# Reordering the steps of an attention and deformable-convolution kernel, with eleven gather buffers in place of ten

## The chip, the cores and the metric

The kernel runs on one core of a Trainium2 chip. Time is device microseconds (us) from the start to the end of one execution, lower is better. Five engines matter: TensorE (PE in the profile, its weight loads PEld), VectorE (DVE), ScalarE (ACT), GpSimd (POOL), which here does nothing but issue indirect DMAs, and SyncE (SP), which issues the plain DMAs.[...]

## The reference

`x` has shape (8, 256, 64, 64) in float32. Two layers follow each other, both of the form `x = x + layer(group_norm(x))`, with 32 groups of 8 channels.

```python
# layer 0: local attention, 4 heads, 3x3 neighbourhood
qkv = einsum('oc,bchw->bohw', w_qkv, x); q, k, v = split(qkv, 3)
logits[b,h,kk,l] = sum_d q[b,h,d,l] * patch3x3(k)[b,h,d,kk,l]
attn = softmax(logits, axis=kk)
kernel[b,h,kk,l] = sum_c w_kg[h,kk,c] * qkv[b,h,c,l] + b_kg[h,kk]   # generated weights
out = w_proj @ (alpha * sum_kk kernel * patch(v) + beta * sum_kk attn * patch(v))

# layer 1: modulated deformable 3x3 convolution
om = conv3x3(x, w_off) + b_off              # 18 offsets and 9 masks a pixel
v  = bilinear sample of x at the 9 shifted places (4 corners each), times sigmoid(mask)
out = einsum('bckhw,ock->bohw', v, w)
```

## The kernel before

**Tiles.** An image is worked on in 8 chunks (`NC`) of 8 rows, 512 pixels each (`N`), with 256 channels as two halves of 128 partitions (`NT`). The current image lies in SBUF as `image`; its value after layer 0 is also stored to DRAM as `kept`.

**Layer 0** is the generator `attention(b)` (L550). It computes the group statistics (`Norm` and `ready`), normalises chunk by chunk (`normed`, tile `xn`), and takes seven steps a chunk, each ended by a `yield`. In step 1 `spread_weights` (four matmuls `wk`, each followed by a DVE multiply L483) belongs to the chunk before, called `d`, and `q(0)`, `q(1)` (L276) belong to this one. Step 2 is `k`, step 3 `products` (the DVE multiply `qk` L354) and half of `weighted`, step 4 logits and `generated`, step 5 `v(0)` and `turned` (`gt`, L398), step 6 `v(1)`, the projection's first half and `softmax_3`, step 7 the projection's second half, `second_stats`, `weights` (transposes of the weights, L462) and `keys(0)` (transposes of v, L498). All of them take PSUM tiles from one pool of four, `ps_a`.

**Between the layers** the generator `prepare(b)` (L617) writes the normalised image to a DRAM table (`to_table`, L629 to L638), computes the offsets (`om`, L649), turns them into table indices and corner weights (`positions`, tiles `idx` and `wt`), loads the next image chunk by chunk, and takes its first statistics (`first_stats`, L258).

**Layer 1** is a loop of slots: one slot is one of the 9 kernel taps of one chunk, so 72 slots an image (`SLOTS`) and 576 in all. A slot needs four blocks of 128 pixels. A block is gathered by an indirect DMA of 128 rows of 4 KB (`gather`, L764, POOL), its first corner is scaled on ACT (`scale`, L780), and the other three are added on DVE (`sum_corners`, L788, three instructions a block). Then PE transposes the block (`transposes`, L815), ACT copies it out of PSUM (L818), and PE multiplies it by the tap's weights into `po` (`product`, L832). After the ninth tap, `finished` (L840) adds `po` to the residual `r` on DVE (L843, two instructions) and stores the result. `po` has a single buffer, so the first product of the next chunk has to wait until `finished` has read it.

**The order.** PE, ACT, DVE and POOL run in the order in which the program is written out by hand (`manual_schedule`). The call `ahead(i)` issues the scaling of blocks i+8 and i+9, the sums of blocks i+6 and i+7, and two gathers. Gathers run `LEAD` = 18 blocks ahead, and only 14 ahead in the last image (`LAST_GATHERS`); they land in a pool of 10 buffers. The loop body for slot n is:

```python
transposes(n); ahead(4 * n)
product(n - 1)
# steps of attention / prepare of the next image, 73 over 72 slots
if the product was a chunk's last: finished(...)
ahead(4 * n + 2)
```

All 73 steps of image 0 and six steps of image 1 (`STEPS + STEPS_AHEAD`) run before the loop; the loop then stays six steps ahead of the image.

Of the kernel before, what the change touches and what calls it, by code (L numbers as in the profile page):

```python
# [58 lines left out]
def preact_kernel(ctx: ExitStack, tc: tile.TileContext, a: dict, out: bass.AP):  # L59
# [75 lines left out]
    for t in xn2:  # L135
        nc.gpsimd.memset(t, 0.0)

    kt = const.tile([P, NT, R + 2, WP], F32, tag="k", name="k")
    vt = const.tile([P, NT, TC, KT, KT], F32, tag="v", name="v")


    w_effT = const.tile([P, NT, HEADS, KK], F32, tag="w_effT", name="w_effT")
    nc.vector.tensor_scalar(bkg, bkg, alpha, None, ALU.mult)
    with (
        tc.tile_pool(name="prep", bufs=1) as prep,
        tc.tile_pool(name="prep_ps", bufs=1, space=PSUM) as prep_ps,
    ):
        ps = prep_ps.tile([P, NT, HEADS, KK], F32, tag="eff", name="eff")
        for ct in range(NT):
            for h in range(HEADS):  # L150
                for i in range(2):
                    nc.tensor.matmul(
                        ps[:, ct, h, :],
                        w_qkv[h // 2][:, 2 * (h % 2) + i, ct * P : (ct + 1) * P],
                        w_kgT[:, 2 * h + i, :],
                        start=(i == 0),
                        stop=(i == 1),
                    )
        for ct in range(NT):
            nc.vector.tensor_scalar(  # L160
                w_effT[:, ct], ps[:, ct], alpha, None, ALU.mult
            )
# [29 lines left out]
    class Norm:  # L192


        def __init__(self, stats, name):
            self.name = name
            mv = p1.tile([P, NT, 2], F32, tag="mv", name=f"mv_{name}")
            for ct in range(NT):
                nc.vector.bn_aggr(mv[:, ct, :], stats[:, ct].rearrange("p c s -> p (c s)"))
            ps = psum_a(f"gn_{name}")  # L200
            nc.tensor.matmul(ps[:, 0:NT], gmat, mv[:, :, 0], start=True, stop=True)
# [48 lines left out]
        return t[:, ct, dy : dy + R, dx : dx + W]  # L250

    stats0: dict = {}

    def first_stats(b, c):
        if c == 0:
            stats0[b] = p2.tile([P, NT, NC, 6], F32, tag="stats0", name=f"stats0_{b}")
        for ct in range(NT):
            nc.vector.bn_stats(  # L258
                stats0[b][:, ct, c, :], image[:, ct, c * N : (c + 1) * N]
            )  # L260

    class Attention:

# [34 lines left out]
                    vt[:, :, :, R : R + 2, :].rearrange("p c t y x -> p (c t) (y x)"),  # L298
                )

        def keyed(self, which, i, to):

            for lo, hi in [(0, 2)] * (self.c == 0 and i == 0) + [(2 + 4 * i, 6 + 4 * i)]:
                for m in range(NT):
                    ps = psum_a(f"ps{'qkv'[which]}_{self.u}_{lo}_{m}")
                    o = which * C + m * P
                    for ct in range(NT):
                        nc.tensor.matmul(  # L308
                            ps[:, : (hi - lo) * WP],
                            w_qkvT[:, ct, o : o + P],  # L310
                            self.xn[:, ct, lo:hi, :],
                            start=(ct == 0),
                            stop=(ct == NT - 1),
                        )
                    to(m, lo, hi, ps)

        def k(self, i):
            self.keyed(
                1,
                i,  # L320
                lambda m, lo, hi, ps: nc.scalar.copy(  # L321
                    kt[:, m, lo:hi, :].rearrange("p r w -> p (r w)"), ps[:, : (hi - lo) * WP]
                ),
            )

        def v(self, i):
            self.keyed(
                2,
                i,
                lambda m, lo, hi, ps: nc.scalar.copy(vt[:, m, :, lo:hi, :], tiled(ps, hi - lo)),  # L330
            )

        def products(self):

# [41 lines left out]
        def generated(self):  # L376

            ps = psum_a(f"gen_{self.u}")
            n = HEADS * KK
# [8 lines left out]
            self.gs = gs = p1.tile([P, N], F32, tag="gs", name=f"gs_{self.u}")[:n]  # L388
            nc.scalar.copy(
                gs.rearrange("p (t y x) -> p y t x", y=T, x=T),  # L390
                ps[:n].rearrange("p (y t x) -> p y t x", y=T, x=T),
            )

        def turned(self):
            ps = psum_a(f"gt_{self.u}")
            n = HEADS * KK
            for j in range(NB):
                nc.tensor.transpose(  # L398
                    ps[:, j * n : (j + 1) * n], self.gs[:, j * P : (j + 1) * P], ident[:n, :n]
                )  # L400
            self.kb = kb = p1.tile([P, self.G, KK], F32, tag="kb", name=f"kb_{self.u}")
            nc.vector.tensor_add(
                kb.rearrange("p (j h) k -> p j (h k)", j=NB),
                ps[:, : NB * n].rearrange("p (j k) -> p j k", j=NB),
                bkg.unsqueeze(1).to_broadcast([P, NB, n]),
            )

# [142 lines left out]
    def attention(b):  # L550

        xt = image
        gn = Norm(stats0.pop(b), f"0_{b}")
        stats = p2.tile([P, NT, NC, 6], F32, tag="stats", name=f"stats1_{b}")
        yield None
        gn = gn.ready()
# [52 lines left out]
        for m in range(NT):  # L609
            d.add(m, d.project(m))  # L610
        d.second_stats()
        yield None
        gn = Norm(stats, f"1_{b}")
        yield None
        yield gn.ready()

    def prepare(b, gn):  # L617
# [24 lines left out]
        def offsets(c, xn):  # L642
# [3 lines left out]
            for k in range(KK):  # L646
                for ct in range(NT):
# [6 lines left out]
                        stop=(n >= KK * NT - 4),  # L654
                    )
                    n += 1
            om = p1.tile([P, N], F32, tag="gs", name=f"om_{b}_{c}")
            nc.scalar.activation(om, ps, AF.Identity, bias=b_off)
            return om

# [131 lines left out]
    def ahead(i):  # L792
# [1 line left out]
        scale(i + SCALE_AHEAD)  # L794
        scale(i + SCALE_AHEAD + 1)
        sum_corners(i + SUM_AHEAD)
        first = (B - 1) * BLOCKS
# [56 lines left out]
    with tc.manual_schedule(engines=ordered):  # L854
# [115 lines left out]
```

## Time and profile before

| | us |
|---|---|
| median of three runs (5568.50, 5571.28, 5586.93) | 5571.28 |
| the profiled execution | 5194.36 |
| its span, first to last instruction | 5192.6 |
| PE busy | 4750.7 (91%) |
| DVE busy | 4182.7 (81%) |
| POOL busy (issuing gathers) | 3151.1 (61%) |
| ACT busy | 2360.6 (45%) |
| mean granted TensorE clock | 0.963 |

The profiled execution took 7% less than the median of the runs. The parts below are worked out in the time of the profiled execution and then carried over to that of the runs. Three stages can be told apart: up to 340 us the steps of image 0 and no gather; from about 370 us to 4735 us slots and steps together; from there to the end the last image's slots alone.

### The profile page before, as it was taken

Reading aid. Unit: us, or ns where it says so; the run is one execution under the profiler, and the core shown is the slowest. Engines: PE = TensorE matmul, PEld = TensorE weight load, DVE = VectorE, ACT = ScalarE, POOL = GpSimd, SP = SyncE. Lnnn points to the kernel's source line nnn. Section 1 sums busy time; section 2 is a strip of 40 time slices with the busy share of each in tenths; the row PEclk is TensorE's granted clock in tenths of the full one; section 3 lists DMA queues with packets and bytes.
Section 4 is the critical chain, followed back from the end, with each engine's and each line's share of the span. In section 5 each row is a group of like instructions: output and inputs, shape, how many; then the busy total and the mean of one; then the engine's idle time right before and its main releaser. Section 6 shows DMA issues by size and latency. Waiting matters only on the chain. (4 is left out here: it accounts for less than half of the span.)

```text
span 5192.6 us, 79716 instructions
## 1 busy us (share of the span) xinstructions
PE 4750.7 (91%) x26592; PEld 2643.4 (51%) x26592; DVE 4182.7 (81%) x10071; ACT 2360.6 (45%) x5184; POOL 3151.1 (61%) x2310
## 2 busy tenths in 40 slices
PE   6979999999999999989999999899999999998888
PEld 4545554555545555455554555445554455544443
DVE  4558788888888888788888888878888888877887
ACT  2334444444444444444444444444444444444544
POOL 0027665666657666566665666746666566666776
PEclk9989999999999999999999999999999999999999
DMA  2058778877797777977779777888778877788998
GB/s 91 21 180 277 266 273 304 300 267 257 275 322 280 268 269 260 337 262 273 279 267 324 273 260 262 287 291 285 268 265 296 297 274 267 267 296 313 388 379 337
DMA packets 476840, 1422.60 MB, mean 274 GB/s; under 512 B 46910, under 2 KB 114750, under 8 KB 476300
## 3 DMA queue, kind: packets, MB, share of 16 engines
q0 software_dynamic: 331776, 1208.11, 65.7%
q1 hardware_dynamic: 141902, 204.27, 11.0%
q10 hardware_dynamic: 2750, 5.12, 0.3%
q8 instruction: 210, 3.44, 0.3%
q14 instruction: 202, 1.65, 0.1%
HBM read 1280.19 MB, written 137.13 MB: 273 GB/s over the span
## 5 line engine op out<-in xcount | busy, mean ns | idle before, releaser
L764 POOL DMA_INDIRECT g<-table,idx x2304 | 3148.6, 1367 | 2019.3 <-DVE s L788 680.7
L788 DVE SCALAR_TENSOR_TENSOR s<-g,wt,s 128x256 f32<-128x256 f32 x6912 | 2798.4, 477 | 418.5 <-ACT s L780 407.4
L832 PE MATMUL po<-vt,w_conv 128*128 128x512 f32 x4608 | 2147.7, 610 | 95.9 <-DVE r L843 95.9
L832 PEld LDWEIGHTS po<-vt,w_conv 128*128 128x128 f32 x4608 | 858.3, 197 | 978.0 <-issue 870.6
L780 ACT ACTIVATE s<-g,wt 128x256 f32<-128x256 f32 x2304 | 1079.8, 509 | 480.6 <-DMA g<-table,idx 412.5
L815 PE MATMUL pt<-ident,s 128*128 128x128 f32 x4608 | 700.4, 285 | 104.1 <-DVE s L788 68.8
L815 PEld LDWEIGHTS pt<-ident,s 128*128 128x128 f32 x4608 | 520.9, 143 | 407.4 <-ACT vt L818 115.6
L818 ACT COPY vt<-pt 128x512 f32<-128x512 f32 x1152 | 610.7, 582 | 125.2 <-PE pt L815 124.7
L276 PE MATMUL psq<-xn,w_qkvT 128*128 128x512 f32 x512 | 301.3, 742 | 91.3 <-DVE wk L483 88.1
L284 ACT COPY q<-psq 128x512 f32<-128x512 f32 x128 | 75.0, 586 | 527.5 <-PE psq L276 527.5
L649 PE MATMUL om<-xn,w_off 128*32 128x512 f32 x2304 | 295.9, 611 | 8.6 <-DVE pos L682 8.6
L308 PE MATMUL psv<-xn,w_qkvT 128*128 128x264 f32 (+1 forms) x1088 | 260.6, 384 | 0.0
L354 DVE TENSOR_TENSOR qk<-qk,near_k 128x400 f32<-128x400 f32 x256 | 129.0, 565 | 161.1 <-PE qk L346 161.1
L276 PEld LDWEIGHTS psq<-xn,w_qkvT 128*128 128x128 f32 x512 | 115.8, 237 | 273.2 <-DVE wk L483 145.9
L308 PE MATMUL psk<-xn,w_qkvT 128*128 128x264 f32 (+1 forms) x1088 | 245.5, 380 | 0.0
L308 PEld LDWEIGHTS psv<-xn,w_qkvT 128*128 128x128 f32 x1088 | 201.7, 192 | 82.8 <-issue 50.1
L528 PE MATMUL proj<-acc,w_projT 128*128 128x512 f32 x512 | 238.2, 592 | 0.7 <-ACT acc L523 0.7
L308 PEld LDWEIGHTS psk<-xn,w_qkvT 128*128 128x128 f32 x1088 | 201.7, 190 | 59.8 <-issue 20.6
L330 ACT COPY v<-psv 128x320 f32<-128x320 f32 (+1 forms) x272 | 110.7, 418 | 249.5 <-PE psv L308 249.4
L321 ACT COPY k<-psk 128x264 f32<-128x264 f32 (+1 forms) x272 | 101.1, 372 | 214.7 <-PE psk L308 214.3
L523 ACT COPY acc<-av 128x512 f32<-128x512 f32 x128 | 74.9, 585 | 256.6 <-PE av L516 256.5
L483 DVE TENSOR_TENSOR wk<-wk,near 100x512 f32<-100x512 f32 x256 | 158.5, 680 | 32.3 <-PE wk L475 32.3
(89 smaller groups left out, 3296.8 us busy)
## 6 DMA issues: line engine op xcount, KB each, us to landing
table<-ts SPq DMA_DIRECT2D x384, 176.0 KB
g<-table,idx POOLq DMA_INDIRECT x2304, 6.3
x<-in_x_dram SPq DMA_DIRECT2D x64, 512.0 KB
x<-x SPq DMA_DIRECT2D x64, 512.0 KB
r<-x SPq DMA_DIRECT2D x64, 512.0 KB
out_dram<-r SPq DMA_DIRECT2D x64, 512.0 KB
w_conv<-in_w_conv_dram ACTq DMA_DIRECT2D x1, 2304.0 KB
w_qkv<-in_w_qkv_dram ACTq DMA_DIRECT2D x2, 384.0 KB
```

The source lines that it names most:

```text
L276: nc.tensor.matmul(ps, w_qkvT[:, ct, m * P : (m + 1) * P], window(self.xn, ct, 4), start=(ct == 0), stop=(ct == NT - 1),)
L308: nc.tensor.matmul(ps[:, : (hi - lo) * WP], w_qkvT[:, ct, o : o + P], self.xn[:, ct, lo:hi, :], start=(ct == 0), stop=(ct == NT - 1),)
L354: nc.vector.tensor_mul(qk[:, 2 * jj : 2 * jj + 2, :, h, :], both[h][:, : 4 * NK].rearrange("p (j c k) -> p j c k", j=2, c=NT), near_k.unsq ...
L483: nc.vector.tensor_mul(wk.rearrange("p (t n) -> p t n", n=T * T), ps[:NK].rearrange("p (t n) -> p t n", n=T * T), near.unsqueeze(1).to_bro ...
L528: nc.tensor.matmul(ps, w_projT[:, ct, m * P : (m + 1) * P], self.acc[:, ct].rearrange("p (t y x) -> p y t x", y=T, x=T), start=(ct == 0), ...
L649: nc.tensor.matmul(ps[32 * g : 32 * g + 32, :], w_off[:, ct, k, :], window(xn, ct, k), start=(n < 4), stop=(n >= KK * NT - 4),)
L764: nc.gpsimd.indirect_dma_start(out=g, out_offset=None, in_=tables[b % 2], in_offset=bass.IndirectOffsetOnAxis(ap=found[b, c][0][:, j, k : ...
L780: nc.scalar.activation(s, g[:, 0:C], AF.Copy, scale=w[:, 0:1])
L788: nc.vector.scalar_tensor_tensor(s, g[:, q * C : (q + 1) * C], w[:, q : q + 1], s, ALU.mult, ALU.add)
L815: nc.tensor.transpose(pt[ct][:, j, :], s[:, ct * P : (ct + 1) * P], ident)
L818: nc.scalar.copy(v[:, ct, :], pt[ct].rearrange("p b n -> p (b n)"))
L832: nc.tensor.matmul(po[:, m, :], w_conv[:, ct, k, m * P : (m + 1) * P], v[:, ct, :], start=(k == 0 and ct == 0), stop=(k == KK - 1 and ct = ...
```

## The change

It makes eight edits in one diff.

1. In step 1 `q(0)`, `q(1)` come ahead of `spread_weights`.
2. In step 7 `keys(0)` comes ahead of `weights`.
3. In the slot that ends a chunk the second `ahead` moves in front of the product, and `finished` follows the product at once, before the steps.
4. `Norm` is split: the aggregation of the statistics (L199) is issued a step earlier, in the step that completes them, and the matmul and what follows become `means()`.
5. The six steps of image 1 no longer run before the loop; the slots of the first image take 79 steps in place of 73.
6. `k` computes 8 rows of 64 columns at once (512 columns, one matmul for each pair of halves) in place of twice 4 rows of 66 columns. The padding columns of `kt` are cleared once at the start.
7. The weights of the generator are padded from 36 to 128 columns with zeros, so `generated` writes 128 partitions and `turned` transposes 128x128 blocks in place of 36x128.
8. Eleven gather buffers and a lead of 19 blocks throughout; the last image is no longer treated apart. To make room, `gs` and `om` share the buffer of `wsb`, and there are 10 in place of 11 buffers for `idx` and `wt`.

```diff
-GATHERS = 10
+GATHERS = 11
-LAST_GATHERS = 6
...
+    nc.gpsimd.memset(kt, 0.0)
...
-    w_effT = const.tile([P, NT, HEADS, KK], F32, tag="w_effT", name="w_effT")
+    w_effT = const.tile([P, NT, P], F32, tag="w_effT", name="w_effT")
+    nc.vector.memset(w_effT, 0.0)
...
-    wp = ctx.enter_context(tc.tile_pool(name="wp", bufs=NC + 3))
+    wp = ctx.enter_context(tc.tile_pool(name="wp", bufs=NC + 2))
...
                 nc.vector.bn_aggr(mv[:, ct, :], stats[:, ct].rearrange("p c s -> p (c s)"))
+
+        def means(self):
+            mv, name = self.mv, self.name
             ps = psum_a(f"gn_{name}")
...
     def first_stats(b, c):
...
+        if c == NC - 1:
+            norm0[b] = Norm(stats0[b], f"0_{b}")
...
+        def k(self, m):
+            for lo, hi in [(0, 2)] * (self.c == 0) + [(2, R + 2)]:
+                ps = psum_a(f"psk_{self.u}_{lo}_{m}")
+                for ct in range(NT):
+                    nc.tensor.matmul(
+                        ps[:, : (hi - lo) * W],
+                        w_qkvT[:, ct, C + m * P : C + (m + 1) * P],
+                        self.xn[:, ct, lo:hi, 1 : W + 1],
+                        start=(ct == 0),
+                        stop=(ct == NT - 1),
+                    )
+                nc.scalar.copy(
+                    kt[:, m, lo:hi, 1 : W + 1],
+                    ps[:, : (hi - lo) * W].rearrange("p (r w) -> p r w", w=W),
+                )
...
                 nc.tensor.matmul(
-                    ps[:n],
-                    w_effT[:, ct].rearrange("p h k -> p (h k)"),
+                    ps,
+                    w_effT[:, ct],
                     window(self.xn, ct, 4),
...
-                nc.tensor.transpose(
-                    ps[:, j * n : (j + 1) * n], self.gs[:, j * P : (j + 1) * P], ident[:n, :n]
-                )
+                nc.tensor.transpose(ps[:, j], self.gs[:, j * P : (j + 1) * P], ident)
...
-        gn = Norm(stats0.pop(b), f"0_{b}")
+        gn = norm0[b]
+        gn.means()
...
+            a_.q(0)
+            a_.q(1)
             if d:
                 d.spread_weights()
-            a_.q(0)
-            a_.q(1)
...
+            a_.keys(0)
             a_.weights()
-            a_.keys(0)
...
         d.second_stats()
+        gn = Norm(stats, f"1_{b}")
         yield None
-        gn = Norm(stats, f"1_{b}")
+        gn.means()
...
-        for n in (i + LEAD, i + LEAD + 1):
-            if n < first:
-                gather(n)
-
-        for n in (i + LEAD, i + LEAD + 1):
-            if n - GATHERS + LAST_GATHERS >= first:
-                gather(n - GATHERS + LAST_GATHERS)
+        gather(i + LEAD)
+        gather(i + LEAD + 1)
...
-        while done < STEPS + STEPS_AHEAD:
+        while done < STEPS:
...
+            last = None
+            if n > 0 and n % KK == 0:
+                last = divmod(n // KK - 1, NC)
             if n < B * SLOTS:
                 transposes(*divmod(n, SLOTS))
                 ahead(NB * n)
-            last = None
+                if last:
+                    ahead(NB * n + 2)
             if n > 0:
-                b, h = divmod(n - 1, SLOTS)
-                product(b, h)
-                if h % KK == KK - 1:
-                    last = b, h // KK
-            while (done - STEPS - STEPS_AHEAD) * SLOTS < (n + 1) * STEPS:
+                product(*divmod(n - 1, SLOTS))
+            if last:
+                finished(*last)
+
+            goal = (n + 1) * STEPS + min(n + 1, SLOTS) * STEPS_AHEAD
+            while (done - STEPS) * SLOTS < goal:
                 next(steps, None)
                 done += 1
-            if last:
-                finished(*last)
-            if n < B * SLOTS:
+            if n < B * SLOTS and not last:
                 ahead(NB * n + 2)
```

More of the change, by code (lines that the diff above doesn't have):

```diff
@@ L160, in preact_kernel @@
             nc.vector.tensor_scalar(
-                w_effT[:, ct], ps[:, ct], alpha, None, ALU.mult
+                w_effT[:, ct, : HEADS * KK],
+                ps[:, ct].rearrange("p h k -> p (h k)"),
+                alpha, None, ALU.mult
             )
@@ L196, in __init__ @@
             self.name = name
-            mv = p1.tile([P, NT, 2], F32, tag="mv", name=f"mv_{name}")
+            self.mv = mv = p1.tile([P, NT, 2], F32, tag="mv", name=f"mv_{name}")
             for ct in range(NT):
                 nc.vector.bn_aggr(mv[:, ct, :], stats[:, ct].rearrange("p c s -> p (c s)"))
+        def means(self):
+            mv, name = self.mv, self.name
             ps = psum_a(f"gn_{name}")
@@ L252, in preact_kernel @@
     stats0: dict = {}
+    norm0: dict = {}
     def first_stats(b, c):
@@ L299, in carry_v, with v @@
                 )
-        def keyed(self, which, i, to):
+        def k(self, m):
[13 more added lines that the diff above has]
+                )
+        def v(self, i):
             for lo, hi in [(0, 2)] * (self.c == 0 and i == 0) + [(2 + 4 * i, 6 + 4 * i)]:
                 for m in range(NT):
-                    ps = psum_a(f"ps{'qkv'[which]}_{self.u}_{lo}_{m}")
-                    o = which * C + m * P
+                    ps = psum_a(f"psv_{self.u}_{lo}_{m}")
                     for ct in range(NT):
@@ L309, in keyed @@
                             ps[:, : (hi - lo) * WP],
-                            w_qkvT[:, ct, o : o + P],
+                            w_qkvT[:, ct, 2 * C + m * P : 2 * C + (m + 1) * P],
                             self.xn[:, ct, lo:hi, :],
@@ L314, in keyed @@
                         )
[L315 to L323, printed above, removed]
-            )
[L326 to L331, printed above, removed]
+                    nc.scalar.copy(vt[:, m, :, lo:hi, :], tiled(ps, hi - lo))
         def products(self):
@@ L378, in generated @@
             ps = psum_a(f"gen_{self.u}")
-            n = HEADS * KK
             for ct in range(NT):
                 nc.tensor.matmul(
-                    ps[:n],
-                    w_effT[:, ct].rearrange("p h k -> p (h k)"),
+                    ps,
+                    w_effT[:, ct],
                     window(self.xn, ct, 4),
@@ L387, in generated @@
                 )
-            self.gs = gs = p1.tile([P, N], F32, tag="gs", name=f"gs_{self.u}")[:n]
+            self.gs = p1.tile([P, N], F32, tag="wsb", name=f"gs_{self.u}")
             nc.scalar.copy(
-                gs.rearrange("p (t y x) -> p y t x", y=T, x=T),
-                ps[:n].rearrange("p (y t x) -> p y t x", y=T, x=T),
+                self.gs.rearrange("p (t y x) -> p y t x", y=T, x=T),
+                ps.rearrange("p (y t x) -> p y t x", y=T, x=T),
             )
         def turned(self):
-            ps = psum_a(f"gt_{self.u}")
+            ps = psum_a(f"gt_{self.u}").rearrange("p (j k) -> p j k", j=NB)
             n = HEADS * KK
             for j in range(NB):
-                nc.tensor.transpose(
-                    ps[:, j * n : (j + 1) * n], self.gs[:, j * P : (j + 1) * P], ident[:n, :n]
-                )
+                nc.tensor.transpose(ps[:, j], self.gs[:, j * P : (j + 1) * P], ident)
             self.kb = kb = p1.tile([P, self.G, KK], F32, tag="kb", name=f"kb_{self.u}")
@@ L403, in turned @@
                 kb.rearrange("p (j h) k -> p j (h k)", j=NB),
-                ps[:, : NB * n].rearrange("p (j k) -> p j k", j=NB),
+                ps[:, :, :n],
                 bkg.unsqueeze(1).to_broadcast([P, NB, n]),
@@ L656, in offsets @@
                     n += 1
-            om = p1.tile([P, N], F32, tag="gs", name=f"om_{b}_{c}")
+            om = p1.tile([P, N], F32, tag="wsb", name=f"om_{b}_{c}")
             nc.scalar.activation(om, ps, AF.Identity, bias=b_off)
@@ L796, in ahead @@
         sum_corners(i + SUM_AHEAD)
-        first = (B - 1) * BLOCKS
-        for n in (i + LEAD, i + LEAD + 1):
-            if n < first:
-                gather(n)
-        for n in (i + LEAD, i + LEAD + 1):
-            if n - GATHERS + LAST_GATHERS >= first:
-                gather(n - GATHERS + LAST_GATHERS)
+        gather(i + LEAD)
+        gather(i + LEAD + 1)
     state: dict = {}
```

## The prediction, made before the changed kernel was run

> **What bounds the kernel now.** I read the page first: PE is busy 9 tenths or more in nearly every slice until the last image, where it falls to 8 and the DMA row rises to 9. Then the windows by stage. Their columns are PE, PEld, DVE, ACT and POOL busy with instruction counts, the granted clock, the DMA share and GB/s.
>
> ```profile
> PE   6979999999999999989999999899999999998888
> DMA  2058778877797777977779777888778877788998
> 450.00:4735.00 4285.00, 3988.29 (x22643) 2235.03 (x22642) 3537.21 (x8548) 1989.50 (x4404) 2731.45 (x1957) 0.96 0.80 281
> 4735.00:5187.00 452.00, 395.33 (x1234) 185.44 (x1232) 382.26 (x928) 219.35 (x454) 344.45 (x298) 0.95 0.93 365
> ```
>
> In the loop PE is idle only 297 of 4285 us, DVE 748. PE's order bounds this stage, with DVE not far behind. In the last stage the DMA engines are 93% busy: gathers bound it. Next the waits on PE, then the timeline of one end of a chunk.
>
> ```profile
> PE po L832 <- DVE r L843: 95.9, 48, 4.5
> PE psq L276 <- DVE wk L483: 88.1, 49, 2.2
> PE gn L201 <- DVE mv L199: 70.8, 16, 18.7
> ```
>
> ```profile
> 2568.90 1.27 DVE L843 TENSOR_TENSOR r<-po,r 128x512 f32<-128x512 f32 x2
> ...
> 2570.22 5.40 PE L832 MATMUL po<-vt,w_conv 128*128 128x512 f32 x8 [2.54 <-DVE r L843]
> ...
> 2577.43 3.71 PE L276 MATMUL psq<-xn,w_qkvT 128*128 128x512 f32 x8 [0.77 <-DVE wk L483]
> ...
> 2589.73 3.60 PE L832 MATMUL po<-vt,w_conv 128*128 128x512 f32 x8
> ```
>
> Three waits hold nearly all of PE's idle time (total, times, longest). The timeline shows that a wait costs twice: after 2.54 us of idleness the eight matmuls take 5.40 us, where the same eight take 3.60 us elsewhere. The granted clock says why.
>
> ```profile
> 2570.20:2573.60 3.40, 3.38 (x4) 1.45 (x5) 3.40 (x9) 0.00 (x0) 1.98 (x3) 0.52 1.00 323
> 2590.00:2593.40 3.40, 3.40 (x13) 1.29 (x15) 2.33 (x6) 2.00 (x5) 1.07 (x2) 1.00 0.90 313
> ```
>
> [...] the trace has 111 ns for the generator's 36 columns and 190 for the projection's 128, so the padded generator's load grows by 79 ns, and it lies beside the matmul before it. [...] `r` starts only when the step's additions and statistics ahead of it are through. [...]
>
> **Part by part**, in the time of the profiled execution (5194.36 us).
>
> *q first.* Removed: the wait of 88.1 us, and the slow matmuls after it. Eight psq instructions at full clock take 3.71 us, so 64 chunks need 237 us; the page has 301.3. Of these 64 us the 49 waiting chunks of 64 have 49. Together 137 us. Added: the third and fourth `wk` matmul reuse the PSUM tiles of q and wait for ACT's copies (586 ns). The first two matmuls cover 0.56 of that (a quarter of 1.12 us each), so the bounds are 0 and 0.59 us for 56 chunks, 0 to 33 us; I take 0.2 each, 11. Moved: DVE's multiplies now wait for q too, some 3.5 us longer. Behind them on DVE stand the sums of the second `ahead`, for which the transposes two slots later wait. At 2587 us DVE stands idle 2.83 us in that same stretch, so PE should not feel it. **126 us saved** (60 to 137).
>
> *Final sums.* The wait is 95.9 us, of which the last stage has 4.6; 91 are left. The slow clock: 2147.7 less 576 slots by 3.60 is 74 us, less what the last stage loses to its own gaps (452 by 0.05, 23), so 51. Together 142 us. But the reordering does not put `r` at the front. It leaves ahead of it six more sums (half of 4.83 us, 2.42) and takes away the step's DVE work: at 2568 us that is 0.69 + 1.28, so `r` would come 0.45 later there. Over the run DVE's other work is (4182.7 - 2798.4 - 81.7) / 577, 2.26 us a slot, nearly the same. What is gained on average is that `r` no longer waits through the step's PE work (`kb` sat 1.48 us in front of an `r` at 2490 us). I take 40%, **57 us saved** (from 25 lost, 56 times 0.45, to 142). The store of `r` moves ahead of the step's DMAs on SP, the two gathers ahead of nothing on POOL; both wait for DVE alone. ACT's scaling moves ahead of the step's copies and may hold them up by a late gather: priced in the slower rival.
>
> *Statistics.* 70.8 less the two before the loop (18.7 and 5.1) is 47; the aggregation (2 by 336 ns) then has a whole slot. **45 us saved** (20 to 57, with some slow clock).
>
> *w's transposes last.* PE's wait for `wts` is 17.2 us; `keys(0)` takes 1.04 us in front of it. **12** (0 to 17). `spread_weights` is a slot away and has q ahead of it, so it doesn't wait for the later `wsb`.
>
> *Generator.* 256 transposes of 128 columns (700.4 / 4608, 152 ns of PE busy each) for 36 columns (27.9 / 256, 109): **11 lost** (0 to 14). The matmuls keep their 512 columns.
>
> *k.* 64 chunks by 3.71 us, and 64 short matmuls at about 0.12, is 245 us; before 245.5. **Nothing** on PE (5 either way). ACT saves about 20 us, which is off the path: ACT is 45% busy. The memsets (some 2.4 us on POOL by its own 1196 ns for half that size, a half us on DVE) lie beside the first loads; cover gone, that is their cost.
>
> *Steps ahead.* The first gather is issued at 340.0 us and lands 6.3 later, but its scaling runs at 365.0, behind six steps on ACT. Without them the loop starts some 18 us sooner, and PE later does the 15.1 us that 340 to 365 shows, at a clock of 0.80 there, so 12. **6 saved** (18 saved to 5 lost).
>
> *Gathers.* In the loop PE hardly waits for them. In the last stage 452 by 0.93 leaves at most 32 us; five more gathers in flight at 365 GB/s bring 7 us once. **5 saved** (30 saved to 15 lost). Shared buffers: `gs` is written after the last `wk` matmul has read `wsb`, and `wsb` after `turned`, two steps earlier. Ten `idx` tiles reach back to a chunk long done. No wait there.
>
> Sum: 126 + 57 + 45 + 12 - 11 + 6 + 5 = 239. DVE takes some back. It has 748 idle us in the loop; PE-bound waits of DVE itself (qk, x, kb, pos, wk: 254 us from 944 to 4520 us) make about 304 of them, the longer wait for wk 56 by 3.5, 196 more. That leaves 248 for a gain of about the same size, so DVE becomes almost the second bound. I take a fifth off: **191 us, 5003 us profiled**. The runs' median stands 1.0726 times above the profiled execution, for a reason that the page doesn't show; carried over, 5003 by 1.0726 is **5366 us**, its own range 5260 to 5450.
>
> **Rivals.**
> - *The waits vanish in full* (17%): 88 + 91 + 47 + 17 idle, 100 of slow clock, 18 and 7 at the ends, less 11, is 357 us: 4837 profiled, 5188 us. For it: the slack of DVE at 2587 us. Against: the 0.45 us worked out above.
> - *DVE becomes the bound* (18%): 70 us saved, 5496. For it: the 248 us of room just used up. It decides when DVE has no idle time left in a slot.
> - *The extra 7% of the runs is a slower TensorE that hides the waits*, or the edits cancel (6%): 5571.
> - *Slower* (9%): at the end of each chunk `r` stands behind 18 sums, whose scaling waits on a gather (ACT's wait for gathers: 412.5 us in 357 times, longest 8.8). If `r` comes 4.4 us later than now, 56 times, that is 248 us, DVE's whole room; the wait for `wk` then lands on PE too, and 248 + 196 less the 239 gained and some overlap leaves about 100 lost: 5680. It decides from 4.4 us on. Against it: PE's wait for sums (pt for s) is 68.8 us in all.
>
> **How the numbers follow.** Likeliest 50%; the range 5170 to 5545 holds it, the DVE rival and most of the full gain, 8 in 10. Faster is 50 + 17 + 18, 85%; the same 6%; slower 9%. A measurement of this kernel tells about 0.3% from no change.
>
> **What would show it.** Right: psq no longer waits for `wk` and its busy time falls towards 240 us; `gn` without a wait in the loop; the clock above 0.975; DVE's wait for `wk` up by some 190 us; the wait po for `r` about halved, not gone. Wrong: a new wait of PE for sums or `vt` above 100 us, po's wait above 96 us, or a last stage longer than 460 us.

## The result, and the profile after

The changed kernel takes 5724.59 us (median of 4 runs, 5723.5 to 5733.9), the kernel before, beside it, 5579.10 (5568.5 to 5595.28): a ratio of 1.026, interval 1.0235 to 1.0284. It is slower; 5366 was forecast, and even the top of the range, 5545, is passed.

The kernel before stands at one of two levels, which went with the chip (chip 7 was used twice, the others once each): near 5540 us on chips 7, 9 and 14, and near 5184 us on chip 11. The profile from which the prediction was made (5194.36 us) is at the lower level, the timed runs beside it (5571.28) are at the upper one. So the profile after is compared here with a new profile of the kernel before at the upper level, `before_again` (chip 7, span 5529.4 us). The four profiles of the change are all at the upper level and agree, with spans from 5726.9 to 5750.6.

The page of the kernel after, 40 slices of the span: PE busy, granted clock, DMA share.

```profile
span 5732.1 us, 78476 instructions
PE   7888998999898998899988989889988899987777
PEclk9999999998999999999999999989999899998888
DMA  2177668676787767767677676877678677688776
```

DMA is no busier than before while everything takes longer (its share of the loop, the last number but one below, is 0.73 after and 0.76 before), so nothing here points to transfers as the bound of the loop. The windows by stage have the columns that the prediction explains; the second begins when the last indices are computed. After:

```profile
450.00:5146.00 4696.00, 4218.37 (x22263) 2330.75 (x22261) 3529.55 (x8544) 1984.32 (x4296) 2882.40 (x1949) 0.93 0.73 255
5146.00:5728.00 582.00, 424.11 (x1236) 209.34 (x1234) 382.23 (x930) 214.86 (x454) 405.31 (x297) 0.83 0.73 283
```

and of `before_again`:

```profile
450.00:4950.00 4500.00, 4077.55 (x22659) 2297.45 (x22658) 3542.08 (x8563) 2000.63 (x4407) 2749.73 (x1960) 0.95 0.76 268
4950.00:5525.00 575.00, 420.19 (x1232) 208.13 (x1230) 382.45 (x929) 214.49 (x454) 394.79 (x298) 0.85 0.76 287
```

196 of the 203 us come in the loop, where PE issues fewer matmuls than before and is busy 141 us longer. The last stage is slow in both (575 and 582 us, 452 in the first profile), so most of that isn't the change's doing. PE's waits (total, times, longest), after:

```profile
PE qk L354 <- issue: 158.0, 271, 1.5
PE pt L816 <- DVE s L795: 122.3, 132, 11.0
PE pt L816 <- ACT vt L819: 114.2, 28, 11.2
PE av L521 <- issue: 94.2, 169, 1.2
PE po L833 <- DVE r L844: 52.0, 21, 6.9
...
PE gn L208 <- DVE mv L203: 19.6, 2, 17.1
```

and of `before_again`:

```profile
PE po L832 <- DVE r L843: 145.6, 43, 8.5
PE qk L346 <- issue: 103.7, 172, 1.9
PE pt L815 <- ACT vt L818: 99.4, 31, 9.3
PE psq L276 <- DVE wk L483: 83.6, 43, 2.2
PE gn L201 <- DVE mv L199: 57.8, 10, 16.9
```

The three waits that the change aimed at did go or shrink: psq's is no longer in the list, po's fell from 145.6 to 52.0, gn's from 57.8 to 19.6. In their place "issue" grew: PE stands still inside `qk` and `av`, waiting for nothing that the profile shows. Adding busy and idle time of each group, `before_again` to after:

| PE group | before | after | difference | forecast |
|---|---|---|---|---|
| psq and wk | 373.7 + 78.9 | 236.9 + 113.4 | -102 | -126 |
| po | 2341.6 | 2296.6 | -45 | -57 |
| gn | 65.0 | 24.6 | -40 | -45 |
| w, gt, psk | 330.5 | 333.3 | +3 | -1 |
| av | 162.9 | 326.5 | +164 | 0 |
| pt | 905.4 | 1006.4 | +101 | 0 |
| qk | 281.1 | 379.4 | +98 | 0 |
| om and proj | 533.9 | 580.7 | +47 | 0 |

The savings came, 185 us on the lines that the prediction priced (it had 229 there, before its deduction for DVE); 410 us of new time on lines that it left alone swallow them (smaller groups give some 22 back). The timeline of PE shows where one piece of it lies. One chunk after:

```profile
2466.59 3.60 PE L833 MATMUL po<-vt,w_conv 128*128 128x512 f32 x8
2470.12 1.69 PE L354 MATMUL qk<-k,q 64*64 64x100 f32 x50
2472.14 0.42 PE L354 MATMUL qk<-k,q 64*64 64x100 f32 x6 [0.33 <-issue]
2473.58 0.41 PE L354 MATMUL qk<-k,q 64*64 64x100 f32 x4 [1.01 <-issue]
2475.00 0.42 PE L354 MATMUL qk<-k,q 64*64 64x100 f32 x4 [1.02 <-issue]
2476.43 0.50 PE L521 MATMUL av<-wk,vk 100*64 100x64 f32 x4 [1.00 <-issue]
2477.86 0.50 PE L521 MATMUL av<-wk,vk 100*64 100x64 f32 x4 [0.93 <-issue]
2479.28 1.57 PE L521 MATMUL av<-wk,vk 100*64 100x64 f32 x24 [0.92 <-issue]
```

In step 3 PE issues 64 `qk` and 32 `av` matmuls, with one weight load for each. Fifty pass in 1.7 us here; from there on four come in every 1.43 us, until the last 24 run through again. The same burst of the kernel before, in `before_again`:

```profile
2394.20 1.28 PE L346 MATMUL qk<-k,q 64*64 64x100 f32 x47
2395.70 0.41 PE L346 MATMUL qk<-k,q 64*64 64x100 f32 x5 [0.22 <-issue]
2396.45 0.58 PE L346 MATMUL qk<-k,q 64*64 64x100 f32 x12 [0.35 <-issue]
2397.18 1.15 PE L516 MATMUL av<-wk,vk 100*64 100x64 f32 x32
```

Here it slows for a moment and recovers. In the first profile, that of the prediction, the stops weren't there to be seen (busy time and mean ns of one, then the idle time before them):

```profile
L516 PE MATMUL av<-wk,vk 100*64 100x64 f32 x4096 | 149.2, 226 | 0.6 <-DVE wk L483 0.5
...
L346 PE MATMUL qk<-k,q 64*64 64x100 f32 x4096 | 106.2, 249 | 0.0
```

### The profile page after: what moved, and what is told of

Its sections match the earlier page's. It is cut to its first block, busy times and chain, and to the rows that moved or that the text cites. A ratio compares the mean times of both kernels' runs of the same rounds, so it can differ in the third digit from the quotient of the medians.

```text
span 5732.1 us, 78476 instructions
## 1 busy us (share of the span) xinstructions
PE 5006.0 (87%) x26080; PEld 2747.8 (48%) x26080; DVE 4173.8 (73%) x10072; ACT 2349.3 (41%) x5056; POOL 3374.5 (59%) x2311
## 5 line engine op out<-in xcount | busy, mean ns | idle before, releaser
L771 POOL DMA_INDIRECT g<-table,idx x2304 | 3370.8, 1463 | 2329.4 <-DVE s L795 833.0
L833 PE MATMUL po<-vt,w_conv 128*128 128x512 f32 x4608 | 2215.9, 626 | 80.7 <-DVE r L844 52.0
L816 PE MATMUL pt<-ident,s 128*128 128x128 f32 x4608 | 745.4, 300 | 261.0 <-DVE s L795 122.3
L362 DVE TENSOR_TENSOR qk<-qk,near_k 128x400 f32<-128x400 f32 x256 | 135.5, 569 | 505.1 <-remote 458.9
L354 PE MATMUL qk<-k,q 64*64 64x100 f32 x4096 | 216.8, 260 | 162.6 <-issue 158.0
L521 PE MATMUL av<-wk,vk 100*64 100x64 f32 x4096 | 230.2, 260 | 96.3 <-issue 94.2
L508 ACT COPY vk<-vk 100x512 f32<-100x512 f32 x256 | 137.4, 588 | 350.2 <-PE vk L503 347.9
L521 PEld LDWEIGHTS av<-wk,vk 100*64 100x64 f32 x4096 | 189.8, 167 | 165.7 <-issue 137.0
L354 PEld LDWEIGHTS qk<-k,q 64*64 64x64 f32 x4096 | 139.5, 134 | 267.5 <-issue 260.7
L488 DVE TENSOR_TENSOR wk<-wk,near 100x512 f32<-100x512 f32 x256 | 158.8, 682 | 146.3 <-PE wk L480 138.1
L315 PE MATMUL psk<-xn,w_qkvT 128*128 128x512 f32 (+1 forms) x576 | 238.4, 558 | 0.4
L286 PE MATMUL psq<-xn,w_qkvT 128*128 128x512 f32 x512 | 235.3, 601 | 1.6 <-DVE xn L235 1.6
```

Source lines behind the costliest of these rows:

```text
L315: nc.tensor.matmul(ps[:, : (hi - lo) * W], w_qkvT[:, ct, C + m * P : C + (m + 1) * P], self.xn[:, ct, lo:hi, 1 : W + 1], start=(ct == 0), ...
L354: nc.tensor.matmul(both[h][64 * t : 64 * t + 64, n : n + NK], self.qt[r, ct, o * T * T : (o + 1) * T * T], kt[r, ct, :, T * o : T * o + KT ...
L521: nc.tensor.matmul(av[64 * h : 64 * h + 64, g, t * T * T : (t + 1) * T * T], self.vk[:, t, o : o + 64], self.wk[2 * g + h][:, i * n + t * ...
L771: nc.gpsimd.indirect_dma_start(out=g, out_offset=None, in_=tables[b % 2], in_offset=bass.IndirectOffsetOnAxis(ap=found[b, c][0][:, j, k : ...
L816: nc.tensor.transpose(pt[ct][:, j, :], s[:, ct * P : (ct + 1) * P], ident)
L833: nc.tensor.matmul(po[:, m, :], w_conv[:, ct, k, m * P : (m + 1) * P], v[:, ct, :], start=(k == 0 and ct == 0), stop=(k == KK - 1 and ct = ...
```

## The experiments

The expectations name theories by letter. **A**: eleven gathers in flight hold up other traffic (semaphores, instructions). **B**: DVE's order, with `r` behind 18 sums. **C**: q first shifts the gathers into the bursts. **D**: the order of the final sums loses the time. **E**: the wider tiles do. **F**: the session or chip decides. **G**: the length of a dense stretch does it: after some hundred PE instructions few pass at a time (an estimate from the burst above, where 50 `qk` matmuls with a weight load each come before the first stop). **H**: what counts is how long a stretch lies beside the gathers, and not how many matmuls it has.

**The kernel before once more** (`before_again`), unedited.

> The kernel before, once more, for its clock and spans in every run and for a second profile. The profile first taken of it (5192.6 us, clock 0.963) is 7% faster than its runs (5579 us), while the changed kernel's profile (5732.1) agrees with its runs. Theory A, too many gathers in flight hold up semaphores and instruction supply: runs near 5580 us with a clock below 0.95, and the profile either again near 5190 with no wait longer than 11 us, or near 5580 with waits of ACT and DVE on other engines that had long been done. Theory B, the order of DVE's work is the cause and the runs merely differ from the profile by a slower TensorE clock: runs near 5580 and a profile with the same waits as before, each a little longer.

5540.93 us, ratio 0.9993 (0.9979 to 1.0007) to the kernel before. The 7% between the first profile and the runs is no trait of profiled executions: this one has a span of 5529.4 us, with the stops.

**The gathers.** The change with ten buffers and six for the last image as before; the change with eight; the kernel before with ten for the last image.

```diff
 after_g10_6:  GATHERS = 10, LAST_GATHERS = 6 and the two loops of ahead() as before
 after_g8:     -GATHERS = 11
               +GATHERS = 8
 before_last10: -LAST_GATHERS = 6
                +LAST_GATHERS = 10
```

> The changed kernel with the gathers as before: 10 buffers, lead 18, and only 6 in flight in the last image. Theory A (gathers in flight): most of the loss goes, 5250 to 5500 us, the last image back from about 67 us a chunk to about 52. Theory B (the residual add behind 18 sums, DVE as the bound): only the last image gains, some 100 us, so 5600 to 5640.

5735.07 us, 1.0342 (1.0300 to 1.0384).

> The changed kernel with 8 gathers in flight throughout in place of 11. Theory A: faster than the changed kernel by 200 us or more (under 5500), the late semaphores gone or rare. Theory B: slower than with 11, since every gather has less time to land: above 5725.

5714.39 us, 1.0291 (1.0244 to 1.0337).

> The kernel before with 10 gathers in flight in the last image too, in place of 6. Theory A: the last image slows from about 52 us a chunk to 60 or more, so 60 to 120 us slower than before, with everything else as before. Theory B: no difference or a few us faster, since the DMA engines are already busy 93% there.

5539.67 us, 0.9996 (0.9982 to 1.0011). The number of gathers, from 8 to 11, moves nothing that these intervals separate. A forecast 200 us or more for it and falls, and the eighth edit has no gain or loss that shows.

**Single edits, on chip 11.** q first alone in the kernel before; the change with `spread_weights` first again; the order of the final sums alone; k and the generator alone.

```diff
 b_qfirst (before):
-            if d:
-                d.spread_weights()
             a_.q(0)
             a_.q(1)
+            if d:
+                d.spread_weights()
 a_spreadfirst (after): the same lines, the other way round
 b_final (before): the second ahead() ahead of the product, finished() behind it
 b_k_gen (before): k in 512 columns, w_effT padded to 128
```

> The kernel before with one edit alone: q ahead of spread_weights. Theory C (the wait for q is gone, but DVE's multiplies for wk end later, so the gather buffers come free later and the gathers fall into the burst of 64 qk and 32 av matmuls, which then runs at a few matmuls per 0.7 us): slower than before by 60 to 200 us, psq's wait gone, PE's stops inside qk and av up from about 110 to 200 us or more. Theory D (the final sums do it: six more sums ahead of the residual add): faster than before by about 100 us, as the prediction's step had it.

5091.01 us, 0.9813 (0.9795 to 0.9832): faster by 93 us.

> The changed kernel with q put back behind spread_weights, everything else as changed. Theory C: most of the loss goes, 5480 to 5600 us, with stops inside qk and av near those of the kernel before. Theory D: slower still, 5750 to 5850.

5193.21 us, 1.0015 (1.0006 to 1.0024): the other seven edits together bring nothing here, where the prediction had 114 us for them.

> The kernel before with one edit alone: the second ahead moved in front of the product at a chunk's end, and the residual add straight behind the product. Theory C: a gain of 20 to 70 us (the prediction's step), or nothing. Theory D: slower than before by 100 us or more.

5205.77 us, 1.0045 (1.0027 to 1.0063). po's wait does fall, to 61.8 us, but psq's grows to 113.5.

> The kernel before with k in 512 columns and the generator padded to 128 columns, no step moved. By the prediction's steps PE loses 11 us: within 0.5% of before. If it is slower by over 60 us, wider tiles are the cause (theory E: fewer small matmuls leave k's copies later, and the products behind them).

5156.07 us, 0.9943 (0.9926 to 0.9959): faster by 28 us.

Here the kernel before stood at 5184.41 us, and none of these four profiles has a stop of `qk` (at most 1.5 us of idle time). They couldn't explain a loss of 145 us; they raised F.

**The same edit on another chip.** The change again, q first alone again, and the change with the old order of the final sums (chip 9, the kernel before at 5537.55 us).

```diff
 a_oldsums (after):
             if n > 0:
                 product(*divmod(n - 1, SLOTS))
-            if last:
-                finished(*last)
 ...
+            if last:
+                finished(*last)
             if n < B * SLOTS:
                 ahead(NB * n + 2)
```

> The changed kernel again. Runs of the kernel before have come out in two groups, near 5545 us with late semaphores and near 5184 us without any, and all the kernels of one session in the same group. Theory F (the chip on which the session ran decides how much dense bursts of small matmuls cost beside saturated DMA engines): in a session of the 5184 kind the changed kernel is faster than before, 5040 to 5130 us, ratio 0.97 to 0.99; in one of the 5545 kind it is slower again, ratio near 1.03. Theory C alone (the collision costs wherever it happens): slower in both.

5734.17 us, 1.0354 (1.0325 to 1.0383).

> The kernel before with q ahead of spread_weights alone, again. In a session of the 5184 kind 0.98 as measured. In one of the 5545 kind theories C and F want it slower than before, 1.01 to 1.03, with stops inside qk and av.

5762.72 us, **1.0426** (1.0385 to 1.0467), for the same kernel that was 0.9813 on chip 11. This is the central finding: an edit that moves two lines costs 4.3% on one chip and brings 1.9% on another. Alone it loses no less than all eight edits together do on this chip (3.5%). PE's timeline of one burst, on chip 11 (`b_qfirst`):

```profile
2432.61 3.60 PE L832 MATMUL po<-vt,w_conv 128*128 128x512 f32 x8
2436.14 1.64 PE L346 MATMUL qk<-k,q 64*64 64x100 f32 x64
2437.74 1.15 PE L516 MATMUL av<-wk,vk 100*64 100x64 f32 x32
```

and on chip 9 (`b_qfirst_2`):

```profile
2569.93 3.60 PE L832 MATMUL po<-vt,w_conv 128*128 128x512 f32 x8
2573.46 1.27 PE L346 MATMUL qk<-k,q 64*64 64x100 f32 x44
2575.77 0.41 PE L346 MATMUL qk<-k,q 64*64 64x100 f32 x4 [1.03 <-issue]
2577.21 0.62 PE L346 MATMUL qk<-k,q 64*64 64x100 f32 x4 [1.03 <-issue]
2578.64 0.95 PE L346 MATMUL qk<-k,q 64*64 64x100 f32 x12 [0.81 <-issue]
2579.52 1.97 PE L516 MATMUL av<-wk,vk 100*64 100x64 f32 x32
```

The same instructions in the same order: 2.8 us against 8.

> The changed kernel with the order of a chunk's end put back (the second ahead behind the steps, the residual add behind the steps). By itself that edit cost 0.4% in a session of the 5184 kind. There: 15 to 40 us faster than the changed kernel. In a session of the 5545 kind: within 60 us of the changed kernel, since the collision of gathers and bursts comes from q.

5761.08 us, 1.0410 (1.0381 to 1.0439), 27 us above the change on the same chip (the two intervals just touch). With the old order po waits 94.4 us for `r`, with the new one 55.2. The new order gains here, as far as the runs separate them; D and B fall.

**Half the bytes a gather.** Corners 2 and 3 are taken from the data of 0 and 1 (chip 9).

```diff
-        g = gp.tile([P, 4 * C], F32, tag="g", name=f"g_{i}")
+        g = gp.tile([P, 2 * C], F32, tag="g", name=f"g_{i}")
...
-                    s, g[:, q * C : (q + 1) * C], w[:, q : q + 1], s, ALU.mult, ALU.add
+                    s, g[:, q % 2 * C : (q % 2 + 1) * C], w[:, q : q + 1], s, ALU.mult, ALU.add
```

> The changed kernel with half the bytes in every gather (128 rows of 2 KB): corners 2 and 3 are left out of the gather, and their sums read corners 0 and 1 again. PE, DVE and ACT do the same work. If saturated DMA engines hold up the small matmuls (theories C and F), the stops inside qk and av go to near nothing and a run takes under 5200 us in either kind of session. If the stops come from the order of PE's or DVE's own work, they stay.

5678.76 us, one run, 55 below the change on this chip, of the 197 that it had lost. Under 5200 was expected if the traffic holds PE up. The stops of `qk` are 162.2 us and of `av` 94.3, 256.5 together; in the four profiles of the change the sum lies between 248 and 265.

**On chip 7: the change; `av` a slot later; half the `qk` matmuls; gathers of 128 bytes a row.**

```diff
 a_avlate (after): step 3 keeps products(); into step 4, with the logits:
-                d.weighted(0)
+                d.weighted(0)
 a_qkhalf (after): one matmul of 128 columns in place of two of 64
-                        for t in range(2):
-                            o = 2 * (2 * jj + j) + t
...
-                                    self.qt[r, ct, o * T * T : (o + 1) * T * T],
+                                self.qt[r, ct, o * T * T : (o + 2) * T * T],
 a_thin (after):
-        g = gp.tile([P, 4 * C], F32, tag="g", name=f"g_{i}")
+        g = gp.tile([P, C // 8], F32, tag="g", name=f"g_{i}")
... (scaling and sums read one gathered element)
```

> The changed kernel once more, for a session of the other kind. Where the kernel before takes about 5184 us: 5040 to 5130 us (theory F). Where it takes about 5545: 5700 to 5760, as twice before.

5727.59 us, 1.0323 (1.0281 to 1.0366). Its profile has 187.1 us of stops in `qk`, 77.6 in `av` and 33.2 in `pt`; the next three runs are held against it.

> The changed kernel with the 32 av matmuls of step 3 moved to step 4, so that they no longer follow the 64 qk matmuls at once. Theory G ([...] only 8 pass per 0.7 to 1.4 us until the pressure ends): in a session of the 5545 kind the stops inside av fall from some 150 us to under 40, and the kernel gains 60 to 200 us on the changed one. Theory H (the stretch of time beside the gathers counts, not the number of matmuls in a row): within 40 us of the changed kernel. In a session of the 5184 kind: within 20 us of the changed kernel.

5704.37 us, 1.0287 (1.0252 to 1.0321). PE's waits:

```profile
PE qk L354 <- issue: 196.8, 311, 1.6
PE pt L815 <- DVE s L794: 131.5, 134, 11.2
PE pt L815 <- ACT vt L818: 105.7, 20, 11.7
...
PE pt L815 <- issue: 61.9, 113, 5.9
```

`av` alone, 32 matmuls, no longer stops (2.7 us idle in all, 80.0 in `after_3`). The stops inside the transposes grow from 33.2 to 61.9, those of `qk` from 187.1 to 196.8. Busy and idle, `av` takes 149 us less, of which 23 reach the end of the kernel. G had forecast a gain of 60 to 200; 23 is what H allowed.

> The changed kernel with 32 qk matmuls of 128 columns of weights in place of 64 of 64: the second tile of each pair meets the first tile's keys, so the logits are not the reference's. The burst is 64 PE instructions shorter. In a session of the 5545 kind, theory G: the stops inside qk go to near nothing, those inside av are halved, 5550 to 5650 us. Theory H: 5680 us or more. In a session of the 5184 kind: some 30 us less than the changed kernel.

5655.13 us, one run. The waits:

```profile
PE pt L815 <- DVE s L794: 153.1, 131, 10.7
PE av L520 <- issue: 128.7, 186, 1.8
PE pt L815 <- ACT vt L818: 101.5, 15, 11.5
PE pt L815 <- issue: 85.9, 137, 8.1
```

Busy and idle, `qk` takes 132.7 us in place of 410.8 and has no stop left; 72 us of those 278 reach the end of the kernel. G had `av`'s stops halved, and they grew from 77.6 to 128.7.

> The changed kernel with gathers of 128 bytes a row in place of 4 KB; scale and sums read one gathered element spread over the row, so the sampled values are not the reference's. The DMA engines are nearly idle. If the traffic of the gathers holds up PE's small matmuls, a session of the 5545 kind shows no late semaphores, no stops inside qk and av, and about 5000 us or less. If they stay, the traffic is not the cause and PE's own instruction rate is. In a session of the 5184 kind: 4950 to 5100.

5676.30 us, one run. DMA moves 44 GB/s instead of 248, and the waits stay:

```profile
PE qk L354 <- issue: 155.8, 249, 1.7
PE pt L816 <- ACT vt L819: 118.8, 24, 15.4
PE av L521 <- issue: 83.5, 163, 1.7
```

It is 51 us below the change, no more than with half the bytes, and the stops of `qk` and `av` together are 239.3 us, near the 248 of the lowest profile of the change. Bytes don't cause the stops: C and H fall as far as the traffic goes. The number of gathers and of their rows is the same in both experiments, so an influence of their number is not excluded.

**Last: the change on one more chip, and the edits that take no wait from in front of the bursts** (chip 14, the kernel before at 5541.13 us).

```diff
 b_kgen_stats (before): k and the generator as after; Norm split, means(); keys(0) ahead of weights().
 q, the final sums, the steps ahead and the gathers as before.
```

> The changed kernel once more, unedited, in a new session. Theory F (the session decides which side q first falls on): if the kernel before comes out near 5545 us, this one is at 5725 to 5745 (ratio 1.03 to 1.037) with the stops of PE inside the qk bursts; if before comes out near 5185, this one is at 5050 to 5150 (0.975 to 0.993), since there q first alone gave 0.981, and the wider k and generator 0.994. Rival: the edits hurt by themselves, wherever it runs: then the ratio is above 1.02 in both kinds of session.

5725.73 us, 1.0328 (1.0310 to 1.0347). The level was the upper one again, so the whole change has no run on chip 11.

> The kernel before with four of the edits: k in 512 columns, the padded generator, the statistics aggregated a step earlier and the transposes of w last; q, the final sums, the steps ahead and the gathers as before. In a session where before is near 5185 us: 28 us for k and the generator as measured, and 40 to 50 more for the wait gn that goes, 5105 to 5125 (0.984 to 0.989). In a session near 5545: if only edits that take a wait from in front of the bursts lose (q first, final sums), this one keeps its gain, 5475 to 5530 (0.987 to 0.997). Rival: any PE time saved is given back inside the bursts there: 0.998 to 1.01.

5516.87 us, **0.9954** (0.9936 to 0.9972): below both kernels, and as expected. The stops of `qk` were 88.3 us (103.7 in `before_again`); without q first they did not grow.

## Why the prediction was wrong

**q first, 126 us saved.** On chip 11 this was nearly right: 93 us, psq at 239.0 us busy and idle, where 237 was forecast. The term that was too small is the added cost: `wk` took 34 us more where 11 was taken and 33 was the upper bound. At the upper level the step has the wrong sign. Alone (`b_qfirst_2` against `before_again`, busy and idle) it saves PE 101 us on psq and wk there too, but loses 95 in `qk`, 124 in `av`, 68 in `pt` and 37 in `po`. That the wait for `wk` is taken away two steps ahead of the burst and the burst then runs worse is what the runs show. Why is not shown. If PE came to the burst with part of G's hundred instructions already behind it, the first stop should come earlier, and it comes later: after 48 `qk` matmuls in the median burst, for 42 in `before_again`. What grows is the number of stops over 0.2 us, from 164 to 255.

**Carrying over by 1.0726.** This is the step that failed: it turned a gain, which `b_qfirst` on chip 11 bears out for q first, into a forecast for runs at the upper level, where q first loses. The factor "for a reason that the page doesn't show" was applied as if it lengthened all work alike and left the differences between two orders alone. It is no factor. In `before_again` the extra time stands in a few places (qk 281.1 us for 106.2, pt 905.4 for 804.5, the last stage 575 for 452), and the edit makes three of them longer (379.4, 1006.4, 582). `qk` and `av` stand in no term of the sum. A profile 7% quicker than the runs that it is to explain showed an execution without the stops. The prediction noted the gap, and asked about it only in a rival of 6%, a slower TensorE that hides the waits; but in `before_again` the waits are there (po 145.6, psq 83.6).

**Final sums, 57 saved.** On chip 11, the level of the profile, wrong: 21 us lost, since psq's and other waits take up what po gives. With the seven edits other than q first at nothing there, the sum of the parts was too high at its own level too: q first brought 93 us where 191 were forecast for all; both together were not run there. On chip 9 the new order of the final sums is worth 27 us. po's wait fell by more than the half that was forecast (145.6 to 52.0). The mechanism of the slower rival, `r` behind 18 sums, did not come true: taking that order away made the kernel slower still. That its 5680 us lie near the result is luck.

**Statistics, w last, 57 saved together; generator 11 lost; k 0.** gn gave 40 us, w 6, and `gt` cost 15. k gave 7 on PE; with the generator it measured 28 us faster on chip 11, where 11 lost was forecast for the two. With the statistics and w last they make 24 us on chip 14.

**Gathers and steps ahead, 11 saved.** The runs with 8, 10 and 11 buffers show nothing; the steps ahead were not tried alone.

**DVE's share, a fifth off.** DVE was busy 4180.0 us in `before_again` and 4173.8 after, of a span 203 us longer. It never became the bound, and that rival falls too. Its idle time in front of `qk`, 505.1 us after for 325.4, fits the stops (158.0 us in `qk` for 103.7): it waits for matmuls that PE brings late, or whose updates come late (counted below).

**The signs that were named.** Of the signs of failure, PE's waits for sums and for `vt`, at 122.3 and 114.2 us (limit 100), and a last stage above 460 appeared. For `vt` and the last stage that was nearly so in `before_again` (99.4 and 575). Of the signs of success, psq (235.3 us busy, no wait for `wk`), `gn` and po came. A clock above 0.975 did not (0.923), and DVE's wait for `wk` rose by 121 us to 146.3, not by 190.

**What stays open** is what the limit on chips 7, 9 and 14 is. G is supported in part at most: shorten a burst, and its own stops end, but they return in what comes next (in `a_qkhalf` the 187.1 us of `qk` go, and the 77.6 of `av` become 128.7), and two of its forecasts failed. One hint speaks against PE's density alone. In the first 330 us, before any gather and before the slots, eight bursts of 64 run through in the same execution. After, `qk` in that window:

```profile
L354 PE MATMUL qk<-k,q x512: 243/246/300, 48.2 to 231.1; 64*64 64x100 f32 x171
its engine sat idle before it (us, times) until:
  ACT k L322: 1.3, 8
```

No run here shows the cause. Three facts of the traces narrow the question.

- Only 3 of the 268 stops of over 0.2 us in `qk` (after, from 330 us on) end at an instruction that waits for a semaphore, and in only 24 was a transfer on one of the two queues of kind "instruction" (q8 and q14) under way. Those of q8, 16 KB each, take 0.95 us in the median after and 0.99 in the first profile. So neither a wait for a semaphore nor a slow transfer on these two queues explains most of the stops.
- At the upper level, updates of semaphores are recorded late. PE's matmuls in the kernel before make 4634 of them. The first profile holds all 4634, and 2 stand over 1 us behind the end of PE's last matmul. `before_again` holds 4179, with 134 as late as that, the latest by 8.67 us. After, the matmuls make 4523; 4107 are recorded, 165 as late, the latest by 10.54 us.
- Many are not recorded at all. Over all semaphores the 15 profiles at the upper level hold between 40572 and 51489 updates (after 50262), the 5 at the lower level between 65105 and 65580 (the first profile 65463). In the first 330 us, where the bursts run through, the profile after lacks none of those of PE, DVE and ACT (266, 312 and 195), and none of PE's is late.

Stops, late updates and missing records thus come together, at one level alone and only once the gathers have begun. It is a coincidence in time, and no experiment took it apart. With updates missing, what the profile names as the end of a wait is also less sure at the upper level.

## What to carry to other kernels

When a profile and the timed runs differ by more than their spread, find out first which lines the difference stands on; a price worked out at one level can have the wrong sign at the other. Here a wait removed from PE was gained only where the burst behind it ran through (q first alone: 0.981 with 2.8 us for the burst shown, 1.043 with 8): look at the densest run of short matmuls behind it, and price it as a term of its own. Edits that need fewer instructions (k in 512 columns) or a result earlier (the statistics) were no loss where they were run, 28 us gained by k and the generator on chip 11 and 24 by them with the statistics and w last on chip 14. Two edits that only reorder work, q first and the final sums (21 us lost on chip 11, 27 gained on chip 9), changed sign from one level to the other.

## What was not expected of the hardware

- The same kernel takes 5184 us on one chip and 5538 to 5546 on three others, and one reordering gives a ratio of 0.981 on the former and 1.043 on one of the latter.
- Where PE stops in a burst, it first does so after 41 to 56 short matmuls (after, median 50; 22 to 58 in `before_again`, median 42). In the worst stretches it then passes four in each 1.43 us, as the timelines above show.
- A result can be noticed very late. In the last stage after, where nothing but slots run, the transposes ended at 5421.35 us, ACT copied them only from 5433.93 on, and PE stood for 9.79. PE had ended its last matmul at 5424.78; seven updates of its semaphore are recorded from 5428.88 to 5433.98:

```profile
5420.31 1.04 PE L816 MATMUL pt<-ident,s 128*128 128x128 f32 x8
...
5433.93 1.07 ACT L819 COPY vt<-pt 128x512 f32<-128x512 f32 x2 [10.83 <-remote]
...
5434.57 2.24 PE L816 MATMUL pt<-ident,s 128*128 128x128 f32 x8 [9.79 <-ACT vt L819]
```

  In the last stage PE waits for `vt` for 114.2 us after, 83.7 in `before_again` and 13.3 in the first profile, the largest part of why this stage takes 582 and 575 us and not 452. Thinner gathers don't end such waits (PE's longest wait for `vt` was 15.4 us with 128 bytes a row).
